# A four-layer convolution block on one core: box sums from row pairs, and strips for three batches made during the last batch's layer 1

## The chip, the cores and the metric

The kernel runs on one core of a Trainium2 chip. The metric is the device time of one execution in microseconds (us); before the change it is 5321.84 us, the median of three runs (5321.01 to 5334.33). A core has five engines that matter here: TensorE (PE, with its weight loads as PEld), VectorE (DVE), ScalarE (ACT), GpSimd (POOL) and SyncE (SP), which issues transfers. Each works through its own queue in order; they meet through semaphores. SBUF is the on-chip memory of 128 partitions, PSUM the small memory that TensorE writes.

## The reference, cut to what matters

The input x is 4 batches of 384 channels of 64 x 64 pixels, all fp32. Four layers follow, each as `x = x + layer(group_norm(x))`:

```python
x = x + L0(gn(x))   # attention over 4096 pixels, then a projection
x = x + L1(gn(x))   # 1x1 conv, filter in the Fourier domain of 8x8 tiles, 3x3 depthwise, gate, 1x1 conv
x = x + L2(gn(x))   # depthwise 3x3 and 5x5, batch norms, gates, an MLP of two 1x1 convs
x = x + L3(gn(x))   # depthwise 7x7 with a kernel made for each batch and channel

# L3, cut
kern = gamma * (x_w * w_mix * Nx) + beta      # (b*c, 7, 7)
out = depthwise_conv(x.reshape(1, b*c, h, w), kern, padding=3)
```

Two things of it are used. In layer 2, the depthwise convolutions read the normalised x1 (the result of layer 1) of all four batches. In layer 3, the term `beta` of the kernel is the same for all 49 taps: its share of the convolution is beta times the sum over a 7 x 7 box of the normalised input, where pixels outside the image count as zero. The input is normalised as (x - gm) * r, with gm and r the mean and inverse deviation of its group.

## The kernel before

The kernel is written in a tile framework, which orders the instructions of each engine itself, by the order of the program and by what is ready. The channels are three chunks (j) of 128.

Phase A makes layers 0 and 1. Layer 1 of batch b runs beside the attention of batch b + 1; that of the last batch runs alone:

```python
def phase_a(self):
    ...
    self.big = pool("a_big", 1)          # q, k, v of the attention; also the diagonals below
    self.probs = pool("a_probs", 2)
    self.blk = pool("a_blk", 4)
    self.work = pool("a_work", 2)
    ...
    for b in range(B):
        nxt = self.qkv_tiles() if b + 1 < B else None
        self.side_by_side(b, self.attention(b, q, k4, vt), self.others(b, nxt))
    ...
    for _ in self.layer1(B - 1):         # alone
        pass

def side_by_side(self, b, steps, others):    # 64 steps of attention, the others spread over them
    per_step = ((172 if b else 0) + (42 if b + 1 < B else 0)) / 64
    ...
```

In the last batch's layer 1, three of nine taps of the 3 x 3 convolution are done on TensorE with diagonal matrices (`diag`, PSUM tile `taps_m`), the other six on VectorE; its output matmuls use the PSUM tag "a" of two banks.

Phase B makes the convolutions of layer 2. Its TensorE needs the pixels on the partitions, in strips of two rows. For this each chunk of x1 is loaded, normalised, transposed in blocks of 128 x 128, and copied from PSUM into the strip buffer z, one copy on ScalarE and the next on VectorE:

```python
def to_strips5(self, j, b):
    for part in range(2):
        x = self.bx_p.tile([P, N // 2], F32, ...)          # 128 x 2048
        nc.sync.dma_start(x, self.x1[b][:, j, part * 2048 : (part + 1) * 2048])
        nc.scalar.activation(x, x, AF.Identity, bias=..., scale=...)
        for i in range(4):
            m = self.pm("strip_m")                          # two PSUM banks in turn
            for k in range(4):
                nc.tensor.transpose(m[:, k * P : (k + 1) * P], x[:, at : at + P], self.ident)
            if i % 2: nc.vector.tensor_copy(zv, mv)
            else:     nc.scalar.copy(zv, mv)

# phase_b
for b in range(B):
    self.to_strips5(0, b)        # first chunk, all four batches
self.nets(cp)
for j in range(NJ):
    for c0 in range(0, P, 2):
        self.conv53(j, c0, st)   # reads z
    ...
```

The buffer z is opened after phase A and lies where phase A had its tiles.

Phase G makes layer 3. First it makes x2 and its norm for each batch, and beside that the strips and boxes of chunk 0 of the batch before. Then, for each chunk, the 7 x 7 convolution (`conv7`) runs in 16 rounds, with two steps of the boxes of the next chunk in each round, and the steps that are left after it. A box of one chunk and batch takes four parts of 16 rows of 64, three steps each:

```python
def boxes(self, j, b, x):
    for part in range(4):
        r0 = 16 * part
        edge = above                              # rows of the part above, before they were changed
        if part < 3:
            above = copy of rows r0 + 13 .. r0 + 16        # ScalarE
        # s[i] = row i + row i + 1, 20 rows (19 of sums), GpSimd
        if part == 0: memset two rows; copy one row
        else:         pairs(0, edge rows 0..2, edge rows 1..3, 3)
        n = 17 if part < 3 else 15
        pairs(3, row(x, r0, n), row(x, r0 + 1, n), n)
        ...
        # six rows from three pair sums, VectorE, 16 rows of 64
        nc.vector.tensor_add(h, row(s, 0, 16), row(s, 2, 16))
        nc.vector.tensor_add(h, h, row(s, 4, 16))
        # the seventh row and the mean: h = x + off(k) + h, where k rows lie in the image
        spans = [(0, 16, 7)]
        if part == 0: spans = [(0, 1, 4), (1, 1, 5), (2, 1, 6), (3, 13, 7)]
        for at, n, k in spans if part < 3 else [(0, 13, 7)]:
            nc.vector.scalar_tensor_tensor(hv, row(x, r0 + 3 + at, n), off(k), hv, ALU.add, ALU.add)
        if part == 3:
            for at, k in ((13, 6), (14, 5), (15, 4)):
                nc.vector.tensor_scalar(row(h, at, 1), row(h, at, 1), off(k), None, ALU.add)
        yield
        for q in range(2):
            # 4 transposes into ht_m; ACT copies to ht; 4 matmuls with a band matrix add 7 columns (box_m)
            nc.vector.scalar_tensor_tensor(xq, m, scale, xq, ALU.mult, ALU.add)   # onto x, in place
        ...
```

`off(k)` is -k times the group's mean. When a box is done, x goes to memory as `rest`, and conv7 adds it to its own result (`rest_o`). The factors of conv7 (`toep`) are products of the weights with a band, one third on GpSimd with the band in SBUF, two thirds on VectorE with the band in PSUM.

Of the kernel before, what the change touches and what calls it, by code (L numbers as in the profile page):

```python
# [21 lines left out]
F32 = mybir.dt.float32  # L22
# [6 lines left out]
NJ = 3  # L29
# [190 lines left out]
class _Builder:  # L220
# [204 lines left out]
        nc.vector.tensor_scalar(large, m[0:1, 0:1], limit, None, ALU.is_gt)  # L425
        self.large = large

    def phase_a(self):


        tc, nc = self.tc, self.nc
        with ExitStack() as ctx:
            self.open_psum(ctx, 2)
            cp = ctx.enter_context(tc.tile_pool(name="a_const", bufs=1))
            pool = lambda name, bufs: ctx.enter_context(tc.tile_pool(name=name, bufs=bufs))
            self.big = pool("a_big", 1)
            self.probs = pool("a_probs", 2)
            self.blk = pool("a_blk", 4)
            self.work = pool("a_work", 2)
            self.center = self.const(cp, "center", PD)  # L440
            self.mean96 = self.const(cp, "mean96", PD)
            self.to_coef = self.const(cp, "to_coef")
# [42 lines left out]
            for b in range(B):  # L485
                nxt = self.qkv_tiles() if b + 1 < B else None
                self.side_by_side(b, self.attention(b, q, k4, vt), self.others(b, nxt))
                if nxt is not None:
                    q, k4, vt = nxt
            for _ in self.layer1(B - 1):  # L490
                pass

    def others(self, b, nxt):
# [8 lines left out]

    def side_by_side(self, b, steps, others):

        per_step = ((172 if b else 0) + (42 if b + 1 < B else 0)) / 64
        ahead = 0.0
        for n, _ in enumerate(steps):
            while others is not None and ahead < n * per_step:
                piece = next(others, None)
                if piece is None:  # L510
                    others = None
                else:
                    ahead += piece
        for _ in others or ():
            pass
# [107 lines left out]
    def maxima(self, b):  # L623
# [14 lines left out]
        for i in range(8):  # L638
            mx = self.sm([P, 4, 2], "mx")
            for t in range(4):  # L640
                for u in range(2):
                    s = self.p4("mx_s")
                    for v in range(4):
                        nc.tensor.matmul(
                            s[:, v],
                            lhsT=q[i][32 * v : 32 * v + 32, t * P : (t + 1) * P],
                            rhs=k[u][32 * v : 32 * v + 32, v * 512 : (v + 1) * 512],
                            start=True,
                            stop=True,
                        )  # L650
                    nc.vector.tensor_reduce(mx[:, t, u : u + 1], s.rearrange("p a b -> p (a b)"), AX.X, ALU.max)
            nm = self.sm([P, 4], "nm")
            nc.vector.tensor_reduce(nm, mx, AX.X, ALU.max, negate=True)
            m = self.pm("nm_m")
            for t in range(4):
                nc.tensor.matmul(
                    m[0:1, t * P : (t + 1) * P], lhsT=nm[:, t : t + 1], rhs=self.ident, start=True, stop=True
                )
            row = self.wk("nm_row", "up", 2)
            nc.scalar.copy(row[0:1], m[0:1])  # L660
            for g in range(4):
                nc.sync.dma_start(self.shifts[b][g : g + 1, i * 512 : (i + 1) * 512], row[0:1])

    def attention(self, b, q, k4, vt):
# [27 lines left out]
        def finish(av):  # L692

            xm = self.work.tile([P, NJ, 512], F32, tag="xm", name="xm")
            up = self.wk("av_up", "up", 2)[0 : PD + 1]
            nc.scalar.activation(up, av[0 : PD + 1], AF.Relu)
            rd = self.wk("av_rd", "rd", 1)
            nc.vector.reciprocal(rd[PD : PD + 1], up[PD : PD + 1])
            m = self.pa("rd_m")
            nc.tensor.matmul(m[0:PD, :], lhsT=self.one[PD : PD + 1, :], rhs=rd[PD : PD + 1], start=True, stop=True)  # L700
            nc.vector.tensor_mul(xm[0:PD, 0], up[0:PD], m[0:PD, :])  # L701
            return xm
# [165 lines left out]
    def tap_weights(self):  # L868

        wd = self.vec("w_dw")  # L870
        self.diag = []
        for j in range(NJ):
            t = self.big.tile([P, 4, P], F32, tag="q", name="diag", bufs=9)
            for k in range(TAPS):
                self.nc.gpsimd.tensor_scalar(t[:, k], self.ident, wd[:, 9 * j + k : 9 * j + k + 1], None, ALU.mult)
            self.diag.append(t)
# [51 lines left out]
    def open_strips(self, ctx):  # L928


        pool = ctx.enter_context(self.tc.tile_pool(name="strips", bufs=1))
        self.z_ = pool.tile([P, P * 136 + 4], F32, tag="z", name="z")
        self.tok_last = self.z_[:, 0 : B * N].rearrange("p (b n) -> p b n", n=N)
        self.h2_last = self.z_[:, 0 : NJ * N].rearrange("p (j n) -> p j n", n=N)

    def phase_b(self):
# [4 lines left out]
        with ExitStack() as ctx:  # L941
# [7 lines left out]
            nc.vector.tensor_copy(self.band7_p, self.band7)  # L949
            self.mean256 = cp.tile([P, P], F32, tag="mean256", name="mean256")  # L950
            nc.gpsimd.memset(self.mean256, 1.0 / 256)
            self.z = self.z_[:, 0 : P * 132].rearrange("p (c k b) -> p c k b", k=33, b=B)
            nc.gpsimd.memset(self.z[:, :, 0], 0.0)
            nc.gpsimd.memset(self.z_[:, P * 132 : P * 132 + 4], 0.0)
            self.s3, self.s5, self.s1, self.s0, self.about = (self.coef(k) for k in ("s3", "s5", "s1", "s0", "about"))
            for b in range(B):
                self.to_strips5(0, b)
            self.nets(cp)
            for j in range(NJ):
                st = self.bt_p.tile([P, 2, P, 6], F32, tag="st", name="st", bufs=1)  # L960
# [12 lines left out]
            for _ in self.toks(NJ - 1):  # L973
                pass

    def to_strips5(self, j, b):

        nc = self.nc
        for part in range(2):
            x = self.bx_p.tile([P, N // 2], F32, tag="x", name="in_x1", bufs=4)  # L980
            nc.sync.dma_start(x, self.x1[b][:, j, part * 2048 : (part + 1) * 2048])
            nc.scalar.activation(x, x, AF.Identity, bias=self.n2[:, j, b : b + 1], scale=self.r2[:, j, b : b + 1])
            for i in range(4):
                m = self.pm("strip_m")
                for k in range(4):
                    at = (4 * i + k) * P
                    nc.tensor.transpose(m[:, k * P : (k + 1) * P], x[:, at : at + P], self.ident)
                mv = m.rearrange("p (k c) -> p c k", c=P)
                k0 = 1 + 16 * part + 4 * i
                zv = self.z[:, :, k0 : k0 + 4, b]  # L990
                if i % 2:
                    nc.vector.tensor_copy(zv, mv)
                else:
                    nc.scalar.copy(zv, mv)

    def conv53(self, j, c0, st):

# [313 lines left out]
    def phase_g(self):  # L1311
# [8 lines left out]
        with ExitStack() as ctx:  # L1320
# [23 lines left out]
            for k in ("a_s", "a_b", "b_s"):  # L1344
                setattr(self, k, cp.tile([P, NJ, B], F32, tag=k, name=k))

            self.off = cp.tile([P, NJ, B, 4], F32, tag="off", name="off")


            self.z = self.z_[:, 0 : P * 136].rearrange("p (c k b) -> p c k b", k=34, b=B)  # L1350
# [42 lines left out]
    def x2_of(self, b):  # L1393
# [63 lines left out]
        nc.vector.tensor_mul(self.a_s[:, :, b], gx, r)  # L1457
        nc.vector.tensor_mul(self.a_b[:, :, b], gx, n)
        nc.vector.tensor_mul(self.b_s[:, :, b], self.vec("beta"), r)
        for k in range(4):  # L1460
            nc.vector.tensor_scalar(self.off[:, :, b, k], gm, -4.0 - k, None, ALU.mult)
        yield x

    def to_strips(self, j, b, x):
# [65 lines left out]
    def boxes(self, j, b, x):  # L1530


        nc = self.nc
        off = lambda k: self.off[:, j, b, k - 4 : k - 3]
        scale = self.b_s[:, j, b : b + 1]
        row = lambda t, r, n: t[:, r * W : (r + n) * W]
        above = None
        for part in range(4):
            r0 = 16 * part
            edge = above  # L1540
            if part < 3:

                above = self.sm([P, 4 * W], "edge")
                nc.scalar.copy(above, row(x, r0 + 13, 4))

            s = self.gw_p.tile([P, 20 * W], F32, tag="w", name="box_2")
            h = self.gw_p.tile([P, 16 * W], F32, tag="w7", name="box_7")

            def pairs(i, u, v, n):
                nc.gpsimd.tensor_add(row(s, i, n), u, v)  # L1550

            if part == 0:
                nc.gpsimd.memset(row(s, 0, 2), 0.0)
                nc.scalar.copy(row(s, 2, 1), row(x, 0, 1))
            else:
                pairs(0, row(edge, 0, 3), row(edge, 1, 3), 3)
            n = 17 if part < 3 else 15
            pairs(3, row(x, r0, n), row(x, r0 + 1, n), n)
            if part == 3:
                nc.scalar.copy(row(s, 18, 1), row(x, 63, 1))  # L1560
                nc.gpsimd.memset(row(s, 19, 1), 0.0)
            nc.vector.tensor_add(h, row(s, 0, 16), row(s, 2, 16))  # L1562
            nc.vector.tensor_add(h, h, row(s, 4, 16))  # L1563

            spans = [(0, 16, 7)]
            if part == 0:
                spans = [(0, 1, 4), (1, 1, 5), (2, 1, 6), (3, 13, 7)]
            for at, n, k in spans if part < 3 else [(0, 13, 7)]:
                hv = row(h, at, n)
                nc.vector.scalar_tensor_tensor(hv, row(x, r0 + 3 + at, n), off(k), hv, ALU.add, ALU.add)  # L1570
            if part == 3:
                for at, k in ((13, 6), (14, 5), (15, 4)):
                    nc.vector.tensor_scalar(row(h, at, 1), row(h, at, 1), off(k), None, ALU.add)
            yield
            for q in range(2):
                m = self.pm("ht_m")
# [18 lines left out]
@with_exitstack  # L1595
def tile_conv_preact4(ctx, tc, ins, out):
    k = _Builder(ctx, tc, ins, out)
    k.phase_a()
    with ExitStack() as last:
        k.open_strips(last)  # L1600
        k.phase_b()
        k.phase_ef()
        k.phase_g()
# [19 lines left out]
```

## Time and profile before

| what | value |
|---|---|
| span of the profiled execution | 5341.5 us |
| TensorE busy | 4744.0 us (89%) |
| VectorE busy | 2902.6 us (54%) |
| ScalarE busy | 2056.1 us (38%) |
| GpSimd busy | 709.8 us (13%) |
| strips of layer 2's first chunk | about 2631 to 2675 us |
| first and last matmul of conv7 | 4723.4 and about 5337 us |

How to read the profile: the 40 slices give each engine's busy share in tenths, from left to right over the span; PEclk is the TensorE clock that was granted. A table of windows gives the busy time of each engine in a stretch. A row of a group names the line, the engine, the operation, what it writes and reads with its shape and count, then the busy time in us, the mean ns of one, and the idle time of the engine just before these instructions, with what ended it. A row of the timeline is start, length, engine, line, operation; square brackets hold the idle time before it. Each fp32 matmul shows as two instructions, a transpose as one.

### The profile page before, as it was taken

The numbers are of one execution on the slowest core, as the hardware profiler recorded it, in microseconds if no ns is written. First come the engines' busy times: TensorE is split into PE (matmuls) and PEld (weight loads), VectorE is DVE, ScalarE is ACT, GpSimd is POOL, SyncE is SP. The second block draws the span as 40 slices with busy tenths as digits, with TensorE's granted clock in tenths as the row PEclk, the third lists the DMA queues.
The fourth block names the chain that finished last, engine by engine and source line by source line (L and its number), as shares of the span: only waits on it lengthen the run. The fifth ranks groups of instructions, "written<-read, shape, count | busy, mean of one in ns | idle before, by whom it ended". The sixth has DMA issues, their size and how long they took to land. (4 is left out here: it accounts for less than half of the span.)

```text
span 5341.5 us, 47697 instructions
## 1 busy us (share of the span) xinstructions
PE 4744.0 (89%) x17899; PEld 2617.0 (49%) x17899; DVE 2902.6 (54%) x4916; ACT 2056.1 (38%) x2612; POOL 709.8 (13%) x510
## 2 busy tenths in 40 slices
PE   5999999999999999989798986599999993478889
PEld 2333443334343433344487875244444443478879
DVE  4322465534655345557667987654411116779785
ACT  3444354454445444421334454411133326521330
POOL 1000000000000000000043433000000001144443
PEclk9999999999999999989798988799999995678889
DMA  5210211211111111112347999766544326645664
GB/s 160 64 46 33 79 60 65 74 39 42 59 59 55 43 48 60 53 65 71 137 134 227 304 280 284 239 251 237 199 165 170 147 83 257 240 146 192 206 200 141
DMA packets 467014, 723.21 MB, mean 135 GB/s; under 512 B 17260, under 2 KB 314967, under 8 KB 458839
## 3 DMA queue, kind: packets, MB, share of 16 engines
q1 hardware_dynamic: 327240, 519.44, 29.6%
q10 hardware_dynamic: 114510, 105.99, 5.8%
q0 software_dynamic: 25024, 94.64, 4.5%
q8 instruction: 144, 2.36, 0.2%
q14 instruction: 96, 0.78, 0.0%
HBM read 440.82 MB, written 279.18 MB: 135 GB/s over the span
## 5 line engine op out<-in xcount | busy, mean ns | idle before, releaser
L715 PE MATMUL av<-probs,vt 128*97 128x512 f32 x2048 | 961.9, 604 | 0.0
L684 ACT ACTIVATE probs<-sc_s 128x1024 f32<-128x1024 f32 x512 | 499.4, 1021 | 765.9 <-PE av L715 745.5
L715 PEld LDWEIGHTS av<-probs,vt 128*97 128x97 f32 x2048 | 320.4, 166 | 506.4 <-issue 502.8
L1016 PE MATMUL conv_m<-toep,z 128*128 128x256 f32 x2304 | 509.1, 384 | 12.2 <-ACT d_o L1025 6.6
L900 DVE SCALAR_TENSOR_TENSOR acc<-band,vecs,acc 128x512 f32<-128x512 f32 x696 | 494.1, 746 | 40.8 <-POOL band L861 17.9
L1279 PE MATMUL h_m<-f_h,cm_w_t 128*128 128x512 f32 x1152 | 496.9, 594 | 7.9 <-ACT f_h L1269 7.9
L1016 PEld LDWEIGHTS conv_m<-toep,z 128*128 128x128 f32 x2304 | 441.8, 192 | 78.2 <-issue 12.1
L1519 PE MATMUL conv_m<-toep,z 128*128 128x128 f32 x3072 | 368.5, 281 | 3.7 <-ACT z L1492 1.9
L1230 PE MATMUL h_s<-e_tok,cm_w_t 128*128 128x512 f32 x768 | 362.5, 595 | 5.1 <-DVE e_tok L1215 5.1
L1519 PEld LDWEIGHTS conv_m<-toep,z 128*128 128x128 f32 x3072 | 361.6, 197 | 5.0 <-ACT z L1492 3.2
L1279 PEld LDWEIGHTS h_m<-f_h,cm_w_t 128*128 128x128 f32 x1152 | 219.5, 191 | 285.2 <-issue 273.7
L676 PE MATMUL sc_s<-q,k 32*128 32x512 f32 x2048 | 304.9, 654 | 34.7 <-ACT probs L684 30.4
L1006 POOL TENSOR_TENSOR toep<-w,band 128x1536 f32<-128x1536 f32 x78 | 268.3, 3439 | 393.5 <-PE conv_m L1016 337.2
L823 PE MATMUL t_m<-w_in_t,xb 128*128 128x384 f32 x768 | 282.6, 502 | 6.0 <-ACT band L851 3.8
L755 DVE SCALAR_TENSOR_TENSOR x_res<-proj_m,bn_c,x_res 128x512 f32<-128x512 f32 x96 | 71.6, 746 | 369.3 <-PE proj_m L748 369.2
L748 PE MATMUL proj_m<-xm,w_proj_t 128*128 128x512 f32 x576 | 267.1, 602 | 3.8 <-DVE xm L701 2.7
L1237 ACT COPY e_h<-h_s 128x1024 f32<-128x1024 f32 x96 | 97.2, 1013 | 398.9 <-PE h_s L1230 398.9
L1230 PEld LDWEIGHTS h_s<-e_tok,cm_w_t 128*128 128x128 f32 x768 | 146.5, 191 | 189.4 <-issue 183.7
L1287 DVE BATCH_NORM_STATS2 h_st<-f_h 128x6 f32<-128x512 f32 x72 | 50.0, 694 | 323.4 <-ACT f_h L1286 323.4
L1006 DVE TENSOR_TENSOR toep<-w,band_p 128x1536 f32<-128x1536 f32 x114 | 199.0, 1747 | 36.8 <-PE conv_m L1016 28.4
L823 PEld LDWEIGHTS t_m<-w_in_t,xb 128*128 128x128 f32 x768 | 142.0, 192 | 150.6 <-issue 65.9
L808 DVE TENSOR_SCALAR xb<-xa_in,gn_gm,gn_r 128x128 f32<-128x128 f32 x384 | 111.6, 343 | 183.6 <-PE t_m L823 181.3
(352 smaller groups left out, 6568.5 us busy)
## 6 DMA issues: line engine op xcount, KB each, us to landing
d<-d_o ACTq DMA_DIRECT2D x96, 512.0 KB
c_d<-d SPq DMA_DIRECT2D x96, 512.0 KB
hid<-e_h ACTq DMA_DIRECT2D x16, 3072.0 KB
f_h<-hid SPq DMA_DIRECT2D x16, 3072.0 KB
in_x<-x SPq DMA_DIRECT2D x16, 2048.0 KB
x_res<-in_x SPq DMA_DIRECT2D x32, 768.0 KB
x_in<-in_x SPq DMA_DIRECT2D x96, 256.0 KB
xa<-x_res POOLq DMA_DIRECT2D x32, 768.0 KB, 3.9
```

What stands on the lines that cost most here:

```text
L676: nc.tensor.matmul(s[:, g], lhsT=k4[32 * g : 32 * g + 32, c], rhs=q[i][32 * g : 32 * g + 32], start=True, stop=True,)
L684: nc.scalar.activation(p[:, h * 1024 : (h + 1) * 1024], s[:, 2 * h : 2 * h + 2].rearrange("p a b -> p (a b)"), AF.Exp, scale=0.25,)
L715: nc.tensor.matmul(av[0 : PD + 1, :], lhsT=vt[:, 4 * c + v, :], rhs=p[:, v * 512 : (v + 1) * 512], start=c == 0 and v == 0, stop=c == 7 an ...
L748: nc.tensor.matmul(m, lhsT=self.w_proj[:, j, o * P : (o + 1) * P], rhs=xm[:, j], start=j == 0, stop=j == NJ - 1,)
L808: self.nc.vector.tensor_scalar(xb[:, j].rearrange("p (r c) -> p r c", c=16), x[:, j].rearrange("p (r w c) -> p w r c", w=4, c=16)[:, w], g ...
L823: nc.tensor.matmul(m[:, 0:C], lhsT=xb[:, j], rhs=self.w_in[:, j, :], start=j == 0, stop=j == NJ - 1,)
L900: nc.vector.scalar_tensor_tensor(out, src(j, k), w, done, ALU.mult, ALU.add)
L1006: eng.tensor_tensor(t, self.w53[:, at : at + 192].rearrange("p (m n) -> p m n", n=8).unsqueeze(2).to_broadcast([P, 24, 8, 8]), band.rearra ...
L1016: nc.tensor.matmul(m[:, c * 256 : (c + 1) * 256], lhsT=self.z_[:, at : at + P], rhs=t[:, 12 * c + 4 * i : 12 * c + 4 * i + 4].rearrange("p ...
L1230: nc.tensor.matmul(s[:, v, :], lhsT=w1[:, j, o * P : (o + 1) * P], rhs=t[j][:, v * 512 : (v + 1) * 512], start=j == 0, stop=j == NJ - 1,)
L1279: nc.tensor.matmul(m, lhsT=w2[:, o, j * P : (j + 1) * P], rhs=h[:, o, v * 512 : (v + 1) * 512], start=o == 0, stop=o == 5,)
L1519: nc.tensor.matmul(m[:, ch * P : (ch + 1) * P], lhsT=self.z_[:, at : at + P], rhs=t[:, 8 * c + 2 * i : 8 * c + 2 * i + 2].rearrange("p m a ...
```

## The change

It has two parts, and small moves that they need.

The strips. Phase A's attention buffers (`big`, `probs`) move to the other end of SBUF and are given up when the attention ends; z is opened there at once. From the 21st step of the last batch's layer 1 on, one piece of strips is made at each step: a quarter of a chunk (1024 columns) of batches 0 to 2, with two groups of four transposes each, in the two PSUM banks of tag "a" and the two `xr` buffers of phase A. Phase B then makes only the last batch's strips of the first chunk. The diagonals and two small tiles get other buffers. The attention's companions are spread with 176 units per batch in place of 172.

The boxes. Rows are added in pairs that don't overlap (0 and 1, 2 and 3, ...); `s` holds ten such pair sums for 16 rows in place of 19 overlapping ones, and `t` the sum of three neighbouring pairs, which serves two rows of the result: the row itself needs one more row above or below. Rows beyond the image are pairs of twice the mean, so that one constant, -7 times the mean, serves every row.

```diff
+            attention.close()
+            self.open_strips(strips)
+            layer1, done = self.layer1(B - 1), iter(())
+            for n, _ in enumerate(layer1):
+                if n == 20:
+                    done = self.strips_of(0, range(B - 1))
+                next(done, None)
+            for _ in done:
                 pass
-        per_step = ((172 if b else 0) + (42 if b + 1 < B else 0)) / 64
+        per_step = ((176 if b else 0) + (42 if b + 1 < B else 0)) / 64
-            t = self.big.tile([P, 4, P], F32, tag="q", name="diag", bufs=9)
+            t = self.wk("diag", ("xs", "xs", "lx")[j], 2).rearrange("p (k n) -> p k n", n=P)
 ... (phase_b)
-            for b in range(B):
-                self.to_strips5(0, b)
+            self.to_strips5(0, B - 1)
+    def strips_of(self, j, batches):
+        for b in batches:
+            for q in range(4):
+                x = self.blk.tile([P, NJ, 512], F32, tag="xr", name="in_x1", bufs=2)
+                self.strips5(j, b, x.rearrange("p j n -> p (j n)")[:, 0:1024], q * 8, self.pa)
+                yield
 ... (boxes)
+                above = self.sm([P, 2, W], "edge")
+                nc.scalar.copy(above, pairs_of(x, r0 + 12, 2)[:, :, 1])
+            s = self.gw_p.tile([P, 10, W], F32, tag="w", name="box_2")
+            t = self.gw_p.tile([P, 8, W], F32, tag="w6", name="box_6")
+            lo, hi = 2, 10
             if part == 0:
+                fill(0)                                        # ScalarE: a row of twice the mean
+                lo = 1
             else:
+                nc.scalar.copy(s[:, 0:2], last[:, 8:10])       # two pair sums of the part above
             if part == 3:
+                fill(9)
+                hi = 9
+            xv = pairs_of(x, r0 + 2 * (lo - 1), hi - lo)
+            nc.gpsimd.tensor_add(s[:, lo:hi], xv[:, :, 0], xv[:, :, 1])
+            last = s
+            nc.gpsimd.tensor_add(t, s[:, 0:8], s[:, 1:9])
+            nc.vector.tensor_add(t, t, s[:, 2:10])
+            hv = pairs_of(h, 0, 8)
+            if part == 0:
+                nc.vector.tensor_scalar(hv[:, 0:2, 0], t[:, 0:2], off(6), None, ALU.add)
+            else:
+                nc.vector.scalar_tensor_tensor(hv[:, 0:2, 0], edge, off(7), t[:, 0:2], ALU.add, ALU.add)
+            nc.vector.scalar_tensor_tensor(
+                hv[:, 2:8, 0], pairs_of(x, r0, 6)[:, :, 1], off(7), t[:, 2:8], ALU.add, ALU.add)
+            n = 8 if part < 3 else 6
+            nc.vector.scalar_tensor_tensor(
+                hv[:, 0:n, 1], pairs_of(x, r0 + 4, n)[:, :, 0], off(7), t[:, 0:n], ALU.add, ALU.add)
             if part == 3:
+                nc.vector.tensor_scalar(hv[:, 6:8, 1], t[:, 6:8], off(6), None, ALU.add)
```

## The prediction

> **What bounds the kernel now.** I read the 40 slices of the span first, to see where TensorE is not the limit, then cut the span into stages by the first and last instruction of each, and read the two stages that the change touches in the groups by shape and in the order of time.
>
> The slices (133.5 us each):
>
> ```profile
> PE   5999999999999999989798986599999993478889
> DVE  4322465534655345557667987654411116779785
> PEclk9999999999999999989798988799999995678889
> ```
>
> TensorE is full nearly everywhere. It thins in slices 18 to 20 (the last batch's layer 1 alone, then the strips of layer 2) and from slice 33 on (layer 3), where VectorE is at 6 to 9 tenths. Both parts of the change aim there. The stages, with the columns stretch, length, then busy us and (instructions) of PE, PEld, DVE, ACT, POOL, then granted clock, DMA share, GB/s:
>
> ```profile
> 2360.00:2580.00 220.00, 204.08 (x639) 102.36 (x637) 144.46 (x275) 39.76 (x76) 9.23 (x21) 0.99 0.19 62
> 2580.00:2631.00 51.00, 35.48 (x71) 15.81 (x71) 34.51 (x60) 12.26 (x11) 2.25 (x6) 0.69 0.43 155
> 2631.00:2675.00 44.00, 31.81 (x135) 23.70 (x136) 22.07 (x34) 30.84 (x27) 3.44 (x1) 0.54 0.59 196
> 4410.00:4715.00 305.00, 128.05 (x675) 115.86 (x675) 219.07 (x318) 180.50 (x244) 54.73 (x43) 0.60 0.60 224
> 4715.00:4905.00 190.00, 170.21 (x1390) 165.69 (x1389) 169.11 (x149) 31.76 (x55) 100.34 (x55) 0.94 0.62 196
> 4985.00:5150.00 165.00, 152.52 (x1283) 149.96 (x1282) 152.78 (x130) 22.10 (x45) 98.89 (x50) 0.96 0.54 176
> 5220.00:5341.00 121.00, 116.16 (x1024) 115.97 (x1024) 67.21 (x57) 0.47 (x1) 47.02 (x20) 0.98 0.47 155
> ```
>
> Rows 1 and 2 are the last batch's layer 1: TensorE 93% and VectorE 66% busy in the body, ScalarE 18%. Row 3 is 44 us in which nothing but strips is made. Row 4 makes x2 and the first chunk's strips and boxes (called G1 below); rows 5 and 6 are the 7x7 convolution of chunks 0 and 1 with the boxes of the next chunk beside it (G2, G4), where VectorE is 89% and 93% busy; row 7 is the same convolution without boxes: 1024 matmuls in 116 us, 113 ns each, which is TensorE's floor for it.
>
> The groups of row 3:
>
> ```profile
> L987 PE MATMUL strip_m<-ident,in_x 128*128 128x128 f32 x128 | 31.2, 418 | 10.5 <-DVE z L992 5.6 <-ACT z L994 4.5 <-ACT gn_r L301 0.4
> L992 DVE COPY z<-strip_m 128x512 f32<-128x512 f32 x16 | 17.2, 1072 | 19.4 <-PE strip_m L987 19.4
> L994 ACT COPY z<-strip_m 128x512 f32<-128x512 f32 x16 | 17.1, 1066 | 13.1 <-PE strip_m L987 13.1
> L982 ACT ACTIVATE in_x<-in_x,n,r 128x2048 f32<-128x2048 f32 x6 | 12.5, 2082 | 0.0
> ```
>
> Four transposes feed one copy out of a bank, two banks are in turn, and TensorE at clock 0.54 and the copies wait for each other: 32 copies in 42 us.
>
> The boxes beside the convolution (4740 to 4905 us):
>
> ```profile
> L1506 DVE TENSOR_TENSOR toep<-wmix,band_p 128x1024 f32<-128x1024 f32 x41 | 49.1, 1210 | 7.2 <-issue 4.1 <-PE conv_m L1519 3.1
> L1562 DVE TENSOR_TENSOR box<-box 128x1024 f32<-128x1024 f32 x12 | 23.0, 1917 | 0.0
> L1563 DVE TENSOR_TENSOR box<-box,box 128x1024 f32<-128x1024 f32 x12 | 15.7, 1307 | 0.0
> L1570 DVE SCALAR_TENSOR_TENSOR box<-in_x,off,box 128x64 f32<-128x64 f32 x9 | 12.2, 1409 | 0.0
> ```
>
> The same 1024-wide operation takes 1210 ns each time with the band in PSUM, and 1917 on average with both operands in SBUF; a 64-wide one, 267 ns at least over the whole run, takes 1409. VectorE's busy time here is partly waiting. Who it waits for shows in the order of time, and after it what limits the rest of the boxes once the convolution is over:
>
> ```profile
> 4902.67 2.49 POOL L1550 TENSOR_TENSOR box<-in_x 128x1088 f32<-128x1088 f32 x1
> 4903.02 3.02 DVE L1570 SCALAR_TENSOR_TENSOR box<-in_x,off,box 128x832 f32<-128x832 f32 x1
> ...
> 4929.83 1.06 PE L1579 MATMUL ht_m<-ident,box 128*128 128x128 f32 x4
> 4930.99 0.59 ACT L1581 COPY ht<-ht_m 128x512 f32<-128x512 f32 x1 [3.07 <-PE ht_m L1579]
> 4931.62 2.08 PE L1585 MATMUL box_m<-cols,ht 128*128 128x128 f32 x8 [0.73 <-ACT ht L1581]
> ```
>
> The 832-wide operation ends just after GpSimd's pair sum would let go (1.07 us elsewhere). In the tail a half part takes 3.66 us (4929.83 to 4933.49), all of it transposes, copy, matmuls: VectorE isn't in it.
>
> [...]
>
> **Part 1, the strips of three batches.** Removed from the path: row 3 shrinks to one batch of four. What is left of it cannot start before the last batch's norm (about 2632). ScalarE then has two normalisations of 2048 (2 x 2.1 us) and four of the eight copies (4 x 1.07), 8.5 us, VectorE the other four beside it; with the first transposes and the last copy 9 to 10 us. The last block's store takes 6 us (3.9 to 6.1 from issue to landing) from about 2624 and its load some 5 us, so the second half is at hand at 2635 to 2637, hardly later. The 5x5 convolution starts near 2643 in place of 2674.7: **-32 us**. Added to rows 1 and 2: 96 transposes at 0.113 us (11 us of PE), 12 copies on DVE (12.9 us), 12 copies (12.8 us) and 12 normalisations of 1024 (about 1.14 us each, from the activations of that width in layer 3; 14 us) on ACT. ACT has room. PE is 93% and DVE 66% busy and they wait for each other band by band, so I take most of the 11 to 13 us as added length: **+9 us**. Moving the diagonals to other buffers costs nothing (GpSimd made them at 1775 to 1876 us, long ahead). Spreading layer 1 at 176 in place of 172 units brings two output groups of batch 2, now run at half clock after the attention (2334.9 to 2344.9 us), inside it: **-2 us**. Part 1 together: -25 us.
>
> **Part 2, the boxes.** Per box (a chunk of one batch), from uncontended durations: adds 1.216 us at 1024 and 0.68 at 512; the three-operand form 1.28 at 1024, 1.07 at 832, 0.746 at 512, 0.27 at 64, so about 0.60 at 384 and 0.33 at 128; the scalar form 0.244 at 64, about 0.30 at 128.
> Before, on VectorE: parts 2 x 1.216 + 3 x 0.27 + 1.07 = 4.31; twice 2 x 1.216 + 1.28 = 3.71; 2 x 1.216 + 1.07 + 3 x 0.244 = 4.23: 16.0 us. After: 0.68 + 0.30 + 0.60 + 0.746 = 2.33; twice 0.68 + 0.33 + 0.60 + 0.746 = 2.36; 0.68 + 0.33 + 0.60 + 0.60 + 0.30 = 2.51: 9.6 us. **6.4 us less per box, 77 us over 12 boxes.** Waiting: in the window above the box work was 77 us for three boxes (the three groups shown, the wider L1570 with 20.4 and L1573 with 6.1), 26 per box, of which 10 is waiting over 18 instructions. After there are 17 such instructions, against GpSimd operations half as long, so 6 to 9 us; I count 8 us less per box beside the convolution.
> GpSimd: pair sums of 1088 in 2.48 us and of 192 in 0.60, so 2.1 ns per element and 0.2 fixed: 11.8 us per box before; after, 512 takes 1.27 and twice four of them, 10.2 us. ScalarE takes over small copies: 0.6 us more per box.
> How much reaches the end:
> - G1: four boxes, 26 to 32 us of 219 VectorE us in 305. The rest of the stage is chains (norm, gate) that the boxes only partly fill. I take two thirds of 30: **-20 us**.
> - G2: 2.7 of four boxes lie beside the convolution (32 of 48 steps). TensorE's floor is 116 + 2.7 x 8 x (0.45 + 0.9) = 145 us, against about 180 between the first and last conv matmul (4723 to 4904). Its first 50 us wait for the last box of G1 and its trip through memory as well. 2.7 x 8 = 21 us of VectorE, two thirds: **-14 us**.
> - G4: 165 us against 145, so less room: **-10 us**.
> - the two tails: the half-clock chain above stays: **-3 us**.
> Part 2 together: -47 us.
>
> **Sum**: 5321.8 - 25 - 47 = 5250 us.
>
> **Rivals.** (a) TensorE is the bound in G2 and G4 anyway and the chains in G1: then part 2 gives only some 20 us and the time is about 5277. For it: 90% of row 5 and 92% of row 6. Against it: VectorE is as full, and rows 5 and 6 are 20 us or more over the floor. (b) The strips lengthen the last layer 1 by as much as they save: its loads share the queue of the layer's own loads, two buffers are in turn, and the output matmuls share their banks. That costs up to 20 us more: 5270. Against it: the loads are 6.3 MB where DMA is at 0.19. (c) All of VectorE's relief counts, waits vanish, and G2 and G4 fall to the floor: 77 + 25 less, 5215 or below.
>
> **Range and chances.** Central 5250; (a) and (b) together end near 5300, (c) near 5210. Range 5208 to 5300. Over 2% faster means under 5215.4: 0.12; over 2% slower, which none of the paths gives: 0.03; within: 0.85.
>
> **What would show it.** Right: 24 of the 32 strip copies of the first chunk before the last batch's norm and 8 after it, with the first conv53 matmul some 10 us after that norm in place of 42; the body of layer 1 about 9 us longer; VectorE's box work of some 115 us over the run without its waits, for 192 now; TensorE near full in G2 and G4. Wrong: if VectorE stays at 90% in G2, the waiting grew with the number of instructions; if a longer layer 1 swallows the strips; or if another order of instructions moves the attention stage, which this sum leaves at its length.

## The result, and the profile after

The changed kernel takes 5243.62 us, the median of four runs (5237.82 to 5248.69), beside 5324.78 us for the kernel before in four runs, one more than above (5321.01 to 5334.33). The ratio is 0.9845, with a 95% interval of 0.9827 to 0.9863: 81 us less. The two profiled executions, at 5341.5 and 5236.1 us, lie further apart (105 us) than the medians, so a stage taken from one pair of traces may be off by several microseconds; below, stages are taken over several runs.

The busy line and the slices of the changed kernel:

```profile
PE 4687.1 (90%) x17899; PEld 2586.8 (49%) x17899; DVE 2772.2 (53%) x4900; ACT 2064.9 (39%) x2656; POOL 664.2 (13%) x498
...
PE   5999999999999999999798987499999994569889
...
DVE  4322465634655345557676987655421115667665
...
PEclk9999999999999999989898988799999996679999
```

In layer 3 (the last seven slices) VectorE falls from up to 9 tenths to 7 at most, and the granted clock of the last three slices is at 9 tenths, where two of them had 8. The stages of the changed kernel, cut at the same events as in the prediction: stretch, length, then busy us and (instructions) of PE, PEld, DVE, ACT, POOL, then granted clock, DMA share, GB/s.

```profile
2322.00:2550.00 228.00, 214.25 (x734) 110.93 (x733) 154.85 (x286) 62.93 (x98) 9.27 (x21) 1.00 0.26 82
2550.00:2603.50 53.50, 35.70 (x70) 15.72 (x70) 36.11 (x65) 5.55 (x8) 1.65 (x3) 0.64 0.23 75
2603.50:2618.50 15.00, 7.62 (x38) 5.65 (x38) 8.66 (x18) 10.45 (x8) 3.47 (x1) 0.61 0.86 335
4352.00:4659.00 307.00, 137.59 (x671) 124.02 (x672) 192.22 (x310) 182.07 (x257) 46.77 (x42) 0.58 0.60 223
4659.00:4832.00 173.00, 162.14 (x1393) 158.41 (x1392) 129.14 (x151) 33.84 (x67) 86.29 (x53) 0.99 0.66 215
4897.00:5049.00 152.00, 147.38 (x1268) 145.51 (x1267) 116.70 (x131) 21.81 (x49) 83.71 (x49) 0.98 0.57 187
5115.00:5236.00 121.00, 116.06 (x1024) 115.87 (x1024) 67.13 (x56) 0.00 (x0) 47.06 (x20) 0.98 0.47 155
```

Row 1, the body of the last layer 1, carries 95 more matmuls and the strips' copies and is 8 us longer. Row 3, strips alone, is 15 us where it was 44. Row 4, G1, is about as long as before (305 then) with 27 us less VectorE work in it. Rows 5 and 6 are 17 and 13 us shorter; TensorE is 94% and 97% busy in them, VectorE 75% and 77%. Row 7 has not changed.

The strips, in the groups of 2390 to 2603.5 us and of 2603.5 to 2618.5 us:

```profile
L1008 PE MATMUL strip_m<-ident,in_x 128*128 128x128 f32 x96 | 14.2, 277 | 2.4 <-ACT z L1014 2.1 <-ACT in_x L1003 0.3
L1014 ACT COPY z<-strip_m 128x512 f32<-128x512 f32 x12 | 12.9, 1075 | 6.2 <-PE strip_m L1008 6.2
L1012 DVE COPY z<-strip_m 128x512 f32<-128x512 f32 x12 | 12.9, 1072 | 2.2 <-PE strip_m L1008 2.1
```

```profile
L1008 PE MATMUL strip_m<-ident,in_x 128*128 128x128 f32 x32 | 7.4, 398 | 8.7 <-ACT in_x L1003 6.9 <-ACT z L1014 1.8
L1003 ACT ACTIVATE in_x<-in_x,n,r 128x2048 f32<-128x2048 f32 x3 | 6.3, 2088 | 0.5 <-DVE n L808 0.5
```

So 24 of 32 copies are made before the last batch's norm, and 8 after it. The boxes beside the convolution of chunk 0 in the changed kernel (4684 to 4832 us):

```profile
L1526 DVE TENSOR_TENSOR toep<-wmix,band_p 128x1024 f32<-128x1024 f32 x41 | 49.5, 1214 | 10.4 <-PE conv_m L1539 10.4
...
L1586 DVE TENSOR_TENSOR box<-box,box 128x512 f32<-128x512 f32 x12 | 8.2, 687 | 16.1 <-POOL box L1585 16.1
L1591 DVE SCALAR_TENSOR_TENSOR box<-edge,off,box 128x128 f32<-128x128 f32 x9 | 7.8, 862 | 1.0 <-PE ht_m L1606 1.0
L1592 DVE SCALAR_TENSOR_TENSOR box<-in_x,off,box 128x384 f32<-128x384 f32 x11 | 6.7, 609 | 0.0
L1596 DVE SCALAR_TENSOR_TENSOR box<-in_x,off,box 128x512 f32<-128x512 f32 x8 | 5.9, 741 | 0.0
```

In this window the 512-wide instructions now run at the length that they have in this trace where no GpSimd instruction overlaps them (687 and 741 ns on average here, 0.67 to 0.69 and 0.73 to 0.75 us there); the waiting sits in the idle column (16.1 us until GpSimd's sum of two neighbouring pairs is there, to which VectorE adds the third) and in the small edge addition, 862 ns on average against 341 at least. Over all of layer 3 the box sums take VectorE 142 us, with the length that instructions gain beside GpSimd's (the 512-wide addition takes up to 2.82 us where one overlaps it), where they took 267; 44 us of idleness ahead of L1586 is new (5 us ahead of its like before).

### The profile page after: what moved, and what is told of

Same layout as the page of the kernel before. It is cut to its first block, busy times and chain, and to the rows that moved or that the text cites. A ratio compares the mean times of both kernels' runs of the same rounds, so it can differ in the third digit from the quotient of the medians.

```text
span 5236.1 us, 47735 instructions
## 1 busy us (share of the span) xinstructions
PE 4687.1 (90%) x17899; PEld 2586.8 (49%) x17899; DVE 2772.2 (53%) x4900; ACT 2064.9 (39%) x2656; POOL 664.2 (13%) x498
## 4 chain that ended last, share of the span: by engine, by line
PE 73%; DVE 10%; ACT 7%; DMA 5%; issue 3%; POOL 1%; SPq 0%; ACTq 0%; DVEq 0%; POOLq 0%
PE av L724 14%; PE h_m L1299 9%; PE h_s L1250 9%; PE conv_m L1036 6%; PE conv_m L1539 6%; PE sc_s L685 4%; PE proj_m L757 4%; PE t_m L832 4%; DVE acc L909 3%; PE box_m L1612 2%; PE out_m L925 2%; PE back_m L857 2%; PE out_m L924 2%; DMA d<-d_o 1%; PE coef_m L847 1%
## 5 line engine op out<-in xcount | busy, mean ns | idle before, releaser
L1045 ACT COPY d_o<-conv_m 128x512 f32<-128x512 f32 x192 | 110.8, 583 | 252.3 <-PE conv_m L1036 213.6
```

The source lines that it names most:

```text
L1045: nc.scalar.copy(self.d_o[:, :, at : at + 2], mv)
```

## The experiments

There are twelve of them, numbered in the order in which they were made. Times are medians; ratios are to the kernel before on the same chip.

**1 to 4: the parts alone.** Experiment 1 is the kernel before with the new boxes. Experiment 2 is the changed kernel with the old ones. Experiment 3 is the kernel before with the one-number edit, and 4 is the kernel before, unchanged.

```diff
# e1_boxes_only: before, with the changed boxes() and
-        self.off = cp.tile([P, NJ, B, 4], ...)     # -4, -5, -6, -7 times the mean
+        self.off = cp.tile([P, NJ, B, 3], ...)     # -6, -7, 2 times the mean
# e3_spread_only: before, with
-        per_step = ((172 if b else 0) + (42 if b + 1 < B else 0)) / 64
+        per_step = ((176 if b else 0) + (42 if b + 1 < B else 0)) / 64
```

> The kernel before with the new box sums alone. My theory (the two parts add up): layer 3 is 47 to 48 us shorter, so about 5276 us, ratio 0.991, and everything before layer 3 stays. Rival (the strips make room that the boxes need, or the boxes gain less than their stage shows): under 35 us of gain, 5290 or above.

> The changed kernel with the old box sums: strips and the spread of 176 alone. My theory: layer 2 starts about 33 us sooner in undisturbed runs, so about 5291 us, ratio 0.9938; the 24 us by which the attention ended sooner in the one profile of after are chance of the granted clock. Rival: the attention really ends 20 us sooner with this order of instructions, and the time is about 5268.

> The kernel before with 176 in place of 172 units, nothing else. My theory: 2 us, inside what can be measured, 5320 or so. Rival: the better spread is what shortens the attention, 15 to 25 us, about 5302.

> The kernel before, unchanged, for a second profile. My theory: its profiled span is nearer to 5322 than to 5341 us and the last attention matmuls for scores come some 10 to 20 us before 2282 us, which shows how much of the difference in the attention is chance. Rival: it again ends at 2280 us or later, and the change itself moved it.

| kernel | time, us | ratio | 95% interval |
|---|---|---|---|
| 1, boxes only | 5287.3 | 0.9926 | 0.9905 to 0.9948 |
| 2, strips and spread | 5286.99 | 0.9928 | 0.9905 to 0.9951 |
| 3, spread only | 5298.77 | 0.9946 | 0.9926 to 0.9967 |
| 4, before again | 5329.58 | 1.0007 | 0.9993 to 1.0021 |

The kernel before was 5326.06 us beside these four. By the ratios the boxes alone bring 39 us and strips and spread together 38 us. Their sum is near the 81 us of the whole: no interaction shows, with intervals of some 12 us to either side. But 29 of the second 38 us belong to the spread, for which I had 2. The strips are left with about 10 us, which these intervals alone do not tell from nothing; the stages below do. Experiment 1 lies between its two expectations. Experiment 2 came out near the 5291 us that I expected, but by luck: its attention did end sooner (the last score at 2268.0 us), as the rival said, and the strips brought less. In experiment 4 the attention ends at 2280.7 us, as the rival said: the earlier end is no chance of one profile.

The stages, read from the first and last instructions of each: a "score" is a `sc_s` matmul, and the last one marks the end of the attention; "first tap" is the first `taps_m` matmul of the last batch's layer 1. All these times are of starts.

| | 172 units, four runs | 176 units, eight runs |
|---|---|---|
| last score at | 2280.7 to 2282.2 us | 2257.5 to 2273.4 us |
| last score to first tap | 97.5 to 98 us | 82.3 to 83.8 us |
| first two attentions, first score to first score of the third | 1046.9 to 1053.5 us | 1043.0 to 1056.0 us |
| third attention, to first score of the last | 607.4 to 611.7 us | 601.2 to 604.4 us |
| last attention, first to last score | 544.8 to 545.9 us | 535.0 to 535.5 us |

The spread ends the attention earlier, by 7 to 25 us, and takes 15 us out of what is left of layer 1 after it. Some 6 us of the earlier end come from the third attention and 10 from the last, in every run; what scatters is the first two, with either number. In the last attention TensorE is busy for 532.4 of 544.9 us in the kernel before and for 529.7 of 535.4 us in experiment 3, so 7 of the 10 us are idle time of TensorE that is gone. Rows of 20 us around the attention's end, of the kernel before and then of experiment 3:

```profile
2280.00:2300.00 20.00, 19.57 (x55) 7.72 (x55) 16.79 (x26) 10.25 (x12) 1.07 (x2) 1.00 0.24 84
2300.00:2320.00 20.00, 6.17 (x10) 1.65 (x9) 18.59 (x25) 3.79 (x5) 0.73 (x1) 0.64 0.16 54
2320.00:2340.00 20.00, 17.96 (x52) 9.25 (x50) 7.13 (x17) 3.03 (x4) 0.73 (x1) 0.76 0.17 64
2340.00:2360.00 20.00, 18.26 (x44) 10.48 (x43) 7.58 (x29) 2.23 (x4) 0.73 (x1) 0.50 0.35 118
2360.00:2380.00 20.00, 20.00 (x77) 11.73 (x76) 8.75 (x27) 4.88 (x10) 0.35 (x1) 1.00 0.13 40
```

```profile
2260.00:2280.00 20.00, 18.40 (x46) 6.14 (x39) 19.86 (x31) 8.00 (x10) 1.44 (x2) 1.00 0.20 76
2280.00:2300.00 20.00, 15.82 (x32) 6.16 (x31) 13.69 (x19) 2.11 (x3) 0.00 (x0) 0.74 0.13 42
2300.00:2320.00 20.00, 16.15 (x59) 12.20 (x59) 6.46 (x26) 4.50 (x6) 1.45 (x2) 0.58 0.33 118
2320.00:2340.00 20.00, 19.88 (x68) 11.25 (x67) 8.61 (x30) 4.75 (x12) 0.00 (x0) 0.91 0.25 79
```

With 172 units TensorE has a row with 6 us of work, and three rows at a granted clock of 0.50 to 0.76 (0.50 over the prediction's two output groups, 2334.9 to 2344.9 us); with 176 there is no such row, and two rows are that low (0.74 and 0.58). In the kernel before, VectorE is busy nearly all of 2290 to 2310 with taps of layer 1 ahead of the attention's last reciprocal, and TensorE stands for 10.4 us before the matmul that needs it (4.0 us in the changed kernel).

**5 to 8: what is still in the way.** Experiment 5 leaves out the box sums of chunks 1 and 2 (the transposes read x itself, so the output of these chunks is not the reference's). Experiment 6 gives the 24 early strip copies to ScalarE. Experiment 7 gives a third copy of each strip of layer 3 to VectorE, for chunks 1 and 2. Experiment 8 takes 184 units.

```diff
# e5_no_sums
+            if j == 0:
                 ...                                   # s, t, h as in the changed kernel
+            else:
+                h = x[:, r0 * W : (r0 + 16) * W]
# e6_copies_act, strips5, in phase A only
-            if i % 2:
+            if i % 2 and not act:
# e7_third_copy, to_strips
-                if i == 1:
+                if i == 1 or (i == 2 and j):
# e8_spread_184
-        per_step = ((176 if b else 0) + ...
+        per_step = ((184 if b else 0) + ...
```

> The changed kernel with the box sums of chunks 1 and 2 left out: no pair sums, no edges, no seventh row; the transposes read x itself, so the output of those chunks is not the reference's. TensorE's, ScalarE's and the last VectorE step stay. My theory (TensorE is the bound of both convolution stages now): each loses 5 us at most, about 5234 us, and the convolution's matmuls of chunk 1 still take 145 us or more. Rival (VectorE and GpSimd still set the pace): 15 us or more in each, 5215 or below.

> The changed kernel, with all 24 strip copies of the last batch's layer 1 on ScalarE. The taps of that layer take 225 us from first to last with the strips and 217 without. My theory: TensorE's transposes and VectorE's copies share the 8 to 9 us; without VectorE's copies 221 us, about 4 us less in all. Rival (transposes alone): 225 stays. Rival (VectorE alone): 217.

> The changed kernel; in layer 3's strips of chunks 1 and 2 the third copy of each part (384 wide) goes to VectorE as well. ScalarE has 42 us of work there in stages of 38 to 40 us between the last box and the convolution, VectorE 13. My theory: ScalarE sets that stage, so each is 8 us shorter, about 5228 us. Rival (TensorE at half clock, 132 transposes, sets it): under 3 us each, 5238 or above.

> The changed kernel with 184 units in place of 176, so that all companions of the attention are through three steps before it ends. Theory A (what runs after the attention runs alone, at half clock, in a chain): a few us less again, about 5235, the attention's last scores no later than 2258 us. Theory B (the gain from 172 to 176 is chance of the order of instructions): the attention ends anywhere within 20 us of 2260.

| kernel | time, us | ratio | 95% interval |
|---|---|---|---|
| 5, no sums in chunks 1, 2 | 5225.32 | 0.9819 | 0.9800 to 0.9837 |
| 6, strip copies on ScalarE | 5249.86 | 0.9857 | 0.9837 to 0.9877 |
| 7, a third copy on VectorE | 5236.62 | 0.984 | 0.982 to 0.986 |
| 8, 184 units | 5256.36 | 0.9871 | 0.9851 to 0.989 |

The convolution of chunk 1 in experiment 5 is near the prediction's estimate of TensorE's floor:

```profile
4882.00:5028.00 146.00, 144.29 (x1265) 143.36 (x1264) 83.12 (x78) 14.86 (x23) 48.92 (x21) 0.99 0.61 199
```

VectorE is 57% busy, TensorE 99%. The floor worked out in the prediction was 145 us; the changed kernel needs 151.7 us there, so the sums that are left cost 6 us in this stage and VectorE is no longer what bounds it. The time, 5225 us, lies between the two expectations.

In experiment 6 VectorE's share of the early copies is not what lengthens layer 1. From the first to the last `taps_m` matmul, runs without early strips take 216.7 to 217.7 us, runs with them 225.1 to 227.8, and experiment 6 takes 223.9. At most 1 to 4 us are VectorE's copies; the rest stays when they are gone, and the time is no shorter. That fits the rival (the 96 transposes alone), but ScalarE's work grew in this kernel, so its part is not separated from TensorE's.

Experiment 7 does not separate from the changed kernel: from the end of one convolution to the start of the next its trace has 60.9 and 64.0 us, the changed kernel's 64.8 and 66.4, less of a gain than the 8 us of my theory. The clock that the rival put at half was 0.71 and 0.64 in the changed kernel, from the last product of a box to the next convolution (4859.8 to 4897 and 5076.5 to 5115 us). Experiment 8 loses 13 us: after the attention only 74.5 us of layer 1 are left in place of 83, but the attention ends at 2283.4 us again, outside both theories. 184 units are not better than 176.

**9 to 12: the first stage of layer 3, and the spread once more.** Experiment 9 leaves out the sums of chunk 0, and 10 all of chunk 0's box work (x is only stored); their output of this chunk is not the reference's. Experiments 11 and 12 are the changed kernel with 172 and 178 units.

```diff
# e9_no_sums_0: as experiment 5, with
-            if j == 0:
+            if j:
# e10_no_boxes_0, first_chunk
         yield from self.to_strips(0, b, x)
-        yield from self.boxes(0, b, x)
+        self.nc.sync.dma_start(self.rest[0][:, :, b], x.rearrange("p (y n) -> p y n", n=P))
+        yield
# e11_after_172, e12_spread_178: the one number, as in experiment 8
```

> The changed kernel with the box sums of chunk 0 left out as well as their share of VectorE, GpSimd and ScalarE (the transposes read x itself, so chunk 0 of the output is not the reference's). Theory: the stretch from the end of layer 2 to the first 7x7 matmul is four passes over x2, one for each batch, and each is as long as its own chain, boxes or not (the first pass, which has no boxes beside it, took about 79 us of the 320); the stretch stays at 315 to 321 us and the time within 6 us of 5243. Rival: VectorE bounds the stretch after all and the new box form only fell short because something else was slowed; then removing some 35 us of its work there makes the stretch 15 to 30 us shorter and the time 5215 to 5230.

> The changed kernel with all of chunk 0's box work left out (sums, transposes, products with the band, the update of x; x is only stored, so chunk 0 of the output is not the reference's). Theory of four passes: four times 78 us and the last batch's first strips, so the stretch from the end of layer 2 to the first 7x7 matmul is still 300 us or more, and the time 5222 to 5243. Rival (the boxes' chain of TensorE and ScalarE, not the sums, bounds the stretch): it falls to 270 us or less and the time to about 5195.

> The changed kernel with layer 1's spread at 172 units as before the change. If the spread's gain adds to the other parts as it stood alone (0.9946 of the time before, 29 us): 5272, with the last attention score at 2281 to 2284 us. If the strips and boxes need the spread, or use part of it up: 5250 to 5260 or 5280 and more.

> The changed kernel with 178 units. If the gain of 176 is a smooth optimum between 172 (attention ends at 2281 us, 98 us of layer 1 left after it) and 184 (2283 us, 74 us left): attention ends at 2258 to 2266 us and the time is 5235 to 5248. If the gain is a matter of single instructions that happen to fall well at 176: anything from 5230 to 5265, with attention's end jumping to 2270 or more.

| kernel | time, us | ratio | 95% interval |
|---|---|---|---|
| 9, no sums in chunk 0 | 5223.58 | 0.9808 | 0.9783 to 0.9833 |
| 10, no boxes in chunk 0 | 5199.16 | 0.9765 | 0.9745 to 0.9786 |
| 11, 172 units | 5272.22 | 0.9898 | 0.9876 to 0.992 |
| 12, 178 units | 5236.75 | 0.9841 | 0.9818 to 0.9864 |

Experiment 11 takes 29 us away again, just what the spread brought alone, with the last score at 2281.8 us: its share is settled, and it adds. Experiment 12 (last score at 2262.0 us) does not separate from 176. No kernel here that makes the whole output clearly beats the changed one.

Experiments 9 and 10 needed a better mark than the first 7x7 matmul, since conv7's first matmuls run between those of the last box. The first matmul of each batch's gate (`xw_m`) is one: it ends a pass over x2. Passes 2, 3 and 4, then from the fourth gate to the end of conv7 of chunk 0:

| kernel | passes, us | three together | then |
|---|---|---|---|
| before | 65.7, 86.6, 75.4 | 227.7 | 208.8 |
| 1, boxes only | 63.9, 83.4, 82.1 | 229.4 | 191.1 |
| changed | 63.9, 84.7, 84.0 | 232.6 | 189.7 |
| 9, no sums in chunk 0 | 59.9, 72.7, 86.7 | 219.3 | 186.1 |
| 10, no boxes in chunk 0 | 60.7, 70.9, 71.9 | 203.5 | 171.3 |

My theory on G1 fell. It is not four passes of fixed length: experiment 10 shortens three of them by 29 us, and experiment 9 by 13. The times, 5199.16 and 5223.58 us, are near those of the rivals, but the stretch from the first gate to the first 7x7 matmul is only 29 and 12 us shorter than in the changed kernel (258.1 us), less than either rival said. Up to the end of this convolution, leaving the sums out takes 17 us, and leaving out the rest of the box work as well takes 47 us. So the larger part of what the boxes cost here is work that the change does not touch: the transposes and products on TensorE (at a granted clock of about 0.6), the copies on ScalarE, and the update of x on VectorE. Which of these binds is not separated.

## Why the prediction was right, and where its steps failed

The total was right, 5250 against 5243.62, but that it came so close is luck: against the prediction the boxes brought 4 to 8 us less and the strips 7 to 13 us less, and the spread 27 us more.

**Boxes, 47 us predicted: 39 measured alone, 43 as the difference of experiment 2 and the changed kernel.** The stages, as means of the four runs with old boxes and five or more with new ones, do not fall where I put them:

| stage | predicted | measured |
|---|---|---|
| G1 | -20 | about +2 |
| G2, conv7 of chunk 0 | -14 | -14 (179 to 165) |
| G4, conv7 of chunk 1 | -10 | -9 (160 to 151) |
| the two tails, from one convolution to the next | -3 | -14 and -11 (79 to 65, 76 to 65) |

Together the rows give about -46. The G1 step, "two thirds of 30", failed. VectorE's work there did shrink. Two of the rows of VectorE's groups in G1, first before (4410 to 4723 us), then after (4350 to 4665):

```profile
L1562 DVE TENSOR_TENSOR box<-box 128x1024 f32<-128x1024 f32 x14 | 21.6, 1542 | 2.9 <-POOL box L1550 2.6 <-PE ht_m L1579 0.2
L1587 DVE SCALAR_TENSOR_TENSOR x<-box_m,b_s,x 128x512 f32<-128x512 f32 x24 | 17.7, 747 | 13.0 <-PE box_m L1585 12.9
```

```profile
L1614 DVE SCALAR_TENSOR_TENSOR x<-box_m,b_s,x 128x512 f32<-128x512 f32 x24 | 17.9, 747 | 23.2 <-PE box_m L1612 23.2
L1586 DVE TENSOR_TENSOR box<-box,box 128x512 f32<-128x512 f32 x16 | 15.1, 947 | 8.3 <-POOL box L1585 8.3
```

VectorE's busy time in these two windows falls from 222 to 196 us, and its idleness before the two steps grows from 15.9 to 31.5 us: 16 of the 26 us freed turn into waits for the products of TensorE and for GpSimd's sums. The rest is not in these two rows. Why the fourth pass is longer with the new boxes (82 to 84 us, 75 to 77 before) is not settled; experiment 9, without the sums, has 86.7 there, so it is not their length. What binds G1 stays open.

The step on the tails, "the half-clock chain above stays", failed too, and by chance it made good for G1. I read one half part of 3.66 us in which VectorE seemed to have no share. The same chain holds VectorE's sums of the next part, a step further on. The part of each tail from its first to its last product, before and then after (96 products each):

```profile
4906.00:4948.30 42.30, 31.41 (x141) 26.55 (x142) 31.11 (x35) 6.59 (x12) 8.35 (x7) 0.58 0.37 118
5148.00:5182.90 34.90, 22.98 (x142) 18.67 (x143) 30.84 (x35) 6.59 (x12) 8.16 (x6) 0.85 0.45 143
```

```profile
4833.10:4859.80 26.70, 18.66 (x142) 16.05 (x143) 16.65 (x28) 6.70 (x12) 2.54 (x2) 1.00 0.56 187
5049.80:5076.50 26.70, 18.68 (x142) 16.04 (x143) 16.64 (x28) 6.70 (x12) 2.54 (x2) 1.00 0.56 187
```

VectorE has 14 us less in each, and this part is 8 us shorter where the granted clock was 0.85 and 16 us where it was 0.58. VectorE alone in the order of time, before and after:

```profile
4930.08 0.75 DVE L1587 SCALAR_TENSOR_TENSOR in_x<-box_m,b_s,in_x 128x512 f32<-128x512 f32 x1 [0.55 <-PE box_m L1585]
4930.75 1.28 DVE L1570 SCALAR_TENSOR_TENSOR box<-in_x,off,box 128x1024 f32<-128x1024 f32 x1
4933.74 0.75 DVE L1587 SCALAR_TENSOR_TENSOR in_x<-box_m,b_s,in_x 128x512 f32<-128x512 f32 x1 [1.72 <-PE box_m L1585]
4934.41 1.22 DVE L1562 TENSOR_TENSOR box<-box 128x1024 f32<-128x1024 f32 x1
4935.76 1.23 DVE L1563 TENSOR_TENSOR box<-box,box 128x1024 f32<-128x1024 f32 x1
4937.40 0.75 DVE L1587 SCALAR_TENSOR_TENSOR in_x<-box_m,b_s,in_x 128x512 f32<-128x512 f32 x1 [0.42 <-PE box_m L1585]
```

```profile
4838.96 0.75 DVE L1614 SCALAR_TENSOR_TENSOR in_x<-box_m,b_s,in_x 128x512 f32<-128x512 f32 x1 [0.44 <-PE box_m L1612]
...
4841.28 0.75 DVE L1614 SCALAR_TENSOR_TENSOR in_x<-box_m,b_s,in_x 128x512 f32<-128x512 f32 x1
4842.64 0.69 DVE L1586 TENSOR_TENSOR box<-box,box 128x512 f32<-128x512 f32 x1 [0.60 <-POOL box L1585]
4843.61 0.75 DVE L1614 SCALAR_TENSOR_TENSOR in_x<-box_m,b_s,in_x 128x512 f32<-128x512 f32 x1 [0.28 <-PE box_m L1612]
```

Before, a part takes 7.32 us (4930.08 to 4937.40), of which 5.23 are VectorE instructions in sequence, three of them on 1024 elements; after, it takes 4.65 us. The low clock came with the old sums: in the eight tails of the four kernels with the old sums this part has a granted clock of 0.58 to 0.86 and takes 34.9 to 42.3 us; in every tail with the new sums, those of experiment 1 among them, it has 1.00 and takes 26.7 to 27.0 us. Eight products take 1.16 us in place of 2.08. By what mechanism the sums and the clock hang together is not shown. Experiment 5, with no sums at all, leaves the tails at 64.4 and 65.6 us, so the sums have nothing more to give there.

**The strips, 23 us predicted without the spread: about 10 measured as the difference of experiments 2 and 3, 15 of experiments 1 and 11.** The added length of layer 1 was right: +9 predicted, +9 measured (217 to 226 us). The gain after the norm was mis-sized: from the last tap to the first conv53 matmul the runs take 74.8 to 77.9 us without early strips and 51.4 to 51.6 with them, 25 us less in place of 32. The stages leave 16 us. (The prediction read the longest of the four, 77.9 us; their mean is 76.) The step that was off is "the second half is at hand at 2635 to 2637, hardly later". In the order of time, changed kernel:

```profile
2594.61 0.72 POOL L931 DMA_DIRECT2D x<-xa_out  x1 [0.70 <-DVE gn_mv L538]
...
2603.63 2.09 ACT L1003 ACTIVATE in_x<-in_x,n,r 128x2048 f32<-128x2048 f32 x1 [0.45 <-DVE n L808]
...
2604.11 0.32 SPq L1002 DMA_DIRECT2D in_x<-x  x1
...
2610.08 2.09 ACT L1003 ACTIVATE in_x<-in_x,n,r 128x2048 f32<-128x2048 f32 x1
...
2618.61 0.80 PE L1036 MATMUL conv_m<-toep,z 128*128 128x256 f32 x1 [0.93 <-DVE net_st L336]
```

The waits of SyncE's queue from 2585 to 2606 us name what held that load (total, times, longest):

```profile
SPq L1002 <- DMA x<-xa_out: 8.8, 1, 8.8
```

The second half's load waits 8.8 us on its queue for the last block's store. Its row among the DMA issues (KB, then us from issue to landing), before and then after:

```profile
x<-xa_out POOLq DMA_DIRECT2D x1, 768.0 KB, 8.3
```

```profile
x<-xa_out POOLq DMA_DIRECT2D x1, 768.0 KB, 9.4
```

I had taken 6, from the range of the stores before it; but the last store of the kernel before took 8.3 us already, which its trace would have told. The normalisation therefore starts at 2610.08 and not behind the first one at 2605.7, 4.4 us later, and the first matmul comes 15 us after the norm in place of 10.

**The spread, 2 us predicted: 29 measured, with an interval of 0.9926 to 0.9967.** "Brings two output groups inside the attention" was far too small, and my theory that the spread is a detail fell. The warning at the end of the prediction, that another order of instructions might move the attention stage, was what happened. Half of the gain is the shorter rest after the attention (98 to 83 us, of which the wait for the reciprocal is 6), the other half a third and a last attention that are shorter although more work is in them. Why the second half vanishes at 184 units is not settled. There the second, third and last attention take 611, 607 and 539 us, beside 595 to 603, 601 to 604 and 535 with 176; the traces do not show why one order runs better than another.

**The rivals.** (a) is half true: TensorE binds G2 and G4 after the change (94% and 97% busy), and G1 gave nothing; but the tails gave what (a) left out, so the boxes brought 39 us or more and not 20. (b) fell: layer 1 grew by the 9 us counted. (c) was too high, as waits for GpSimd and TensorE took the place of the freed time.

## What to carry to other kernels

A change of one number in how two streams of work are interleaved can be worth more than the work one saves, so test it alone before crediting the rest of the change, and try several values: here 176 and 178 were level, 172 and 184 slower. When an engine is relieved, read for each stage which instruction waits for it last: the gain came where VectorE's sums lay in the loop (the tails, the convolutions) and in G1 it turned into waits for TensorE's products and GpSimd's sums. Before taking a range for a transfer, read the one transfer that lies on the path: the last store was longer than all before it. A low granted clock in a loop need not stay when another engine's work in it changes: in the tails it was 0.58 to 0.86 with the old sums and 1.00 with the new ones, so the chain read at that clock was no floor.

## What the runs showed of the hardware that was not expected

The first two attentions together take anywhere from 1043.0 to 1056.0 us in these traces, with 172 and with 176 units alike, while the last one agrees within 1.1 us for each number: most of the scatter of the last score is made there. The last of the 32 stores of 768 KB took 8.3 us from issue to landing in the kernel before and 9.4 in the changed one, every other such store of these two 3.8 to 5.9 us; in all fourteen traces the last is the longest (8.3 to 9.8 us), and why is not shown. GpSimd's addition of 512 elements takes 1.27 us and VectorE's 0.69 us, and moving one addition from VectorE to GpSimd put 16 us of idleness on VectorE beside one convolution; it can have cost no more than the 6 us or so that experiment 5 gains in such a stage.
